# Building the scan part's diagonals by small transfers, ordering its transfers as written, and moving the skip term to TensorE

## The chip, the cores and the metric

The program runs on one core of a Trainium2 chip, in one launch. The metric is the device time of one execution in microseconds (us). The core's engines each run their own list of instructions in order: PE (TensorE, matrix products), DVE (VectorE), ACT (ScalarE), POOL (GpSimd) and SP (SyncE, which here only issues DMA transfers). Semaphores make one engine wait for another.

## The reference, cut to what matters

Two layers run one after the other on an image of 8 x 128 channels x 128 x 128. The first (Fourier and convolution attention) is untouched by the change. The second is a selective state-space layer over the 16,384 places of each image:

```python
xs, z = split(u @ W_in)                  # u: normalised image, 256 + 256 channels
xc = silu(depthwise_conv4(xs) + conv_b)
dt, Bm, Cm = split(xc @ W_xproj)         # 8, 16, 16 numbers for each place
delta = softplus(dt @ W_dt + b_dt)
# for every place t, 256 channels d, 16 states n:
h[d,n] = exp(delta[d] * A[d,n]) * h[d,n] + delta[d] * xc[d] * Bm[n]
y[d]   = sum_n h[d,n] * Cm[n]
y = (y + xc * D_param) * silu(z)
out = x + y @ W_out
```

`xc * D_param` is the skip term and `silu(z)` is the gate.

## The kernel before, in words

The second layer is the stage at L1025 to L1390, here called the scan part. It works on chunks of T = 512 places, 32 chunks for each of 8 images, 256 in all. A chunk `i` has ST = 16 steps. A step `n` handles one block of 128 partitions (32 channels x 4 groups of states, with 2 states of each group at a time), with h (half of the channels) from s // 8, mp (which pair of states) from s // 4 % 2 and k from s % 4. The steps of one chunk thus use mp = 0, 1, 0, 1 in fours.

In each step the main loop (L1366 to L1390) writes, in this order: `keep_state(n-1)` (ACT copies the last state), `product(n+1)` (PE writes delta * xc * Bm into an `hb` tile in PSUM), the functions of the list `first`, `decay(n+3)` (ACT takes two exponentials `dA`), `scan(n)` (DVE runs two scans of 512 places), the functions of the list `beside`, and `weigh(n)` (POOL multiplies the 2 x 512 results by Cm). An entry `(step, rel, f)` of a list means: in this step call f for chunk i + rel. Entries with rel 1 and 2 prepare later chunks, those with 0 and -1 finish the current and the last one.

`product` (L1239) is 32 small matmuls. Its moving operand `bd` holds, for each block of 64 places, a diagonal matrix with the values of Bm on the diagonal, and its stationary operand is `duT`, the transposed delta * xc. `hb` has two buffers, so `product(n+1)` must wait until `scan(n-1)` is through. A float32 matmul stands in the profile as two MATMUL records, so one product is 64 records.

Before the change the diagonals are made by multiplying the constant `same` (64 x 64 ones on the diagonal) by Bm: six on DVE (`diagonals`, L1198, 128x512 each) and sixteen on ACT (`more_diagonals`, L1210, 128x64 each) for each chunk. `keep_b` (DVE, L1193) keeps a copy of Bm from PSUM.

`add` (L1273) sums over the states on PE: 32 matmuls for each chunk, in groups of four that use different columns of the array, into bank 3 of PSUM (`y`). `skip` (DVE, L1288) then computes xc * D_param + y into `yt` in SBUF, and `gated` (POOL, L1297) multiplies `yt` by the gate `sz`. `project` (PE) and `residual` (DVE) end the chunk.

The other parts of the preparation are `conv` (PE, eight matmuls of 128x512, four taps for each half), `conv_act` (ACT), `gate` (PE and ACT), `xproj` and `xproj_act` (PE and ACT, tile `dbl`), `step_sizes` (PE, tile `e_dt`), `step_sizes_act` (ACT, tile `dl`), `drive` (POOL, tile `du`), `turn` (PE transposes, tile `e_t`) and `turn_b` (PE transposes of Bm, tile `e_bt`).

Some values must be repeated over partitions, which goes through DRAM: `cd` holds Cm and is read back as `crep` (4 transfers of 128 KB for each of the two mp), and `dld` holds delta and is read back as `dlrep` (4 transfers of 256 KB for each half). `xin` is the chunk's input. `acc` is a block of 32 image rows read in pieces of 128 bytes (2 MB, once in 8 chunks); it takes the result, and `out<-acc` writes it back the same way from ACT's queue.

PE, DVE, ACT and POOL are wrapped in `InOrder` (L169), which keeps each engine's instructions in the order in which the program writes them. All their instructions therefore have the helper's line, L180, in the profile. The transfers of SP are not wrapped before the change: the scheduler of the framework chooses their place.

Of the kernel before, what the change touches and what calls it, by code (L numbers as in the profile page):

```python
# [27 lines left out]
T = 512  # L28
# [83 lines left out]
def _layout(a):  # L112
# [46 lines left out]
    o["same64"] = np.tile(np.eye(64, dtype=np.float32), (2, 1))  # L159
# [31 lines left out]
def tile_kernel(ctx: ExitStack, tc: tile.TileContext, I: dict, out: bass.AP):  # L191
# [833 lines left out]
    with tc.tile_pool(name="e_c", bufs=1) as cp, tc.tile_pool(name="e_w", bufs=2) as wk, tc.tile_pool(  # L1025
# [10 lines left out]
        same = fixed("same", [128, ND], I["same64"])  # L1036
        unit = fixed("unit", [128, 128], I["consts"][:, 0:128])
        win = fixed("win", [128, 2 * DI], I["win"])
# [4 lines left out]
        conv_b, b_dt, d_par = dv[:, 0:2], dv[:, 2:4], dv[:, 4:6]  # L1043
        A = fixed("A", [128, NM, NBK], I["alog"])
# [3 lines left out]
        wf = cp.tile([128, 4, DI], F32, name="wf")  # L1048
        nc.sync.dma_start(wf.rearrange("p a d -> p (a d)"), I["cw"].partition_broadcast(128))
        for k in range(4):  # L1050
            nc.vector.tensor_tensor(wf[:, k, :], wf[:, k, :], win[:, 0:DI], ALU.mult)
        state = cp.tile([128, NM, NBK], F32, name="state")
        ch = {}
# [4 lines left out]
        pe, dve, act, gps = (InOrder(tc, e) for e in (nc.tensor, nc.vector, nc.scalar, nc.gpsimd))  # L1058

        def load(i):  # L1060
            b, k = divmod(i, NCH)
            xin = wk.tile([128, T], F32, name="xin")
            nc.sync.dma_start(xin, X1[b, :, k * T : (k + 1) * T])
            ch[i] = {"xin": xin}

        def rows_of(b, r0):

            t = wk.tile([128, W, QR], F32, name="acc")
            nc.sync.dma_start(t, X1[b].rearrange("c (w h) -> c w h", h=H)[:, :, r0 : r0 + QR])
            image[b, r0] = t  # L1070
# [34 lines left out]
        def conv_act(i):  # L1105
            c = ch[i]
            c["xc"] = wk.tile([128, 2, T], F32, name="xc", bufs=3)
            for h in range(2):
                act.activation(c["xc"][:, h, :], c.pop(("xcp", h)), AF.Silu, bias=conv_b[:, h : h + 1])

        def gate(i):
            c = ch[i]
            c["sz"] = wk.tile([128, 2, T], F32, name="sz", bufs=3)
            for h in range(2):
                ps = bank("e_z", h)
                pe.matmul(ps, lhsT=win[:, DI + h * 128 : DI + (h + 1) * 128], rhs=c["u"][:, 3:], start=True, stop=True)
                act.activation(c["sz"][:, h, :], ps, AF.Silu)

        def xproj(i):
            c = ch[i]  # L1120
            ps = c["xp"] = bank("e_x", 0)
            for h in range(2):
                pe.matmul(ps, lhsT=wx[:, h, :], rhs=c["xc"][:, h, :], start=(h == 0), stop=(h == 1))

        def xproj_act(i):
            c = ch[i]
            c["dbl"] = wk.tile([128, T], F32, name="dbl", bufs=1)
            act.copy(paired(c["dbl"]), halves(c.pop("xp")))
            d = c["cd"] = dp.tile([DS, T], F32, name="cd")
            for x in range(2):  # L1130
                nc.sync.dma_start(halves(d)[:, x], paired(c["dbl"][64 + DS : 96, :])[:, x])
            repeat_c(i, 0)

        def repeat_c(i, mp):

            t = ch[i]["c", mp] = wk.tile([128, 2, T], F32, name="crep", bufs=3)
            for q in range(NQ):
                m = NM * q + 2 * mp
                to = t[q * NR : (q + 1) * NR].rearrange("p m t -> p (m t)")
                nc.sync.dma_start(to, ch[i]["cd"][m : m + 2].rearrange("m t -> (m t)").partition_broadcast(NR))  # L1140
# [8 lines left out]
        def step_sizes_act(i):  # L1149
            c = ch[i]  # L1150
            c["dl"] = wk.tile([128, 2, T], F32, name="dl", bufs=1)
            d = dp.tile([2, 128, T], F32, name="dld")
            for h in range(2):
                act.activation(c["dl"][:, h, :], c.pop(("dp", h)), AF.Softplus, bias=b_dt[:, h : h + 1])
            nc.sync.dma_start(d.rearrange("h p t -> p h t"), c["dl"])
            for h in range(2):
                if h:
                    repeat_c(i, 1)
                t = c["dlr", h] = wk.tile([128, 4, T], F32, name="dlrep")
                for q in range(NQ):  # L1160
                    nc.sync.dma_start(t[q * NR : (q + 1) * NR], d[h].rearrange("(k r) t -> r k t", r=NR))
# [7 lines left out]
        def turn(i, part):  # L1169

            c = ch[i]
            ps = c["tp"] = bank("e_t", 1)
# [20 lines left out]
        def keep_b(i):  # L1193
            c = ch[i]
            c["bt"] = wk.tile([128, NTB, DS], F32, name="bt")
            dve.tensor_copy(c["bt"], c["bp"][:, : NTB * 32].rearrange("p (j n) -> p j n", n=32)[:, :, :DS])

        def diagonals(i, mp, j):  # L1198
# [3 lines left out]
            if (mp, j) in ((0, 0), (1, 0)):  # L1202
                c["bd", mp] = wk.tile([128, NTB, NQ, ND, 2], F32, name="bd")
            to = [128, NQ, ND, 2]
            b = c["bp"][:, 32 * j : 32 * j + DS].rearrange("p (q m) -> p q m", m=NM)[:, :, 2 * mp : 2 * mp + 2]
            dve.tensor_tensor(
                c["bd", mp][:, j], same.unsqueeze(1).unsqueeze(3).to_broadcast(to), b.unsqueeze(2).to_broadcast(to), ALU.mult
            )

        def more_diagonals(i, which):  # L1210

            c = ch[i]
            for n in which:
                j, q, m = 2 + n // 8, n // 2 % 4, n % 2
                at = NM * q + 2 + m
                act.activation(c["bd", 1][:, j, q, :, m], same, AF.Identity, scale=c["bt"][:, j, at : at + 1])
# [56 lines left out]
        def add(i, g, *js):  # L1273

            if g % 2 == 0 and 0 in js:
                ch[i]["y", g // 2] = bank("y", 3)
            for j in js:
                for k in range(4):
                    pe.matmul(
                        ch[i]["y", g // 2][k * NR : (k + 1) * NR, :], lhsT=gath, rhs=hcs[ST * i + 4 * g + k][:, j, :],  # L1280
                        start=(g % 2 == 0 and j == 0), stop=(g % 2 == 1 and j == 1), skip_group_check=True,
# [6 lines left out]
        def skip(i, h):  # L1288

            c = ch[i]  # L1290
            if h == 0:
                c["yt"] = wk.tile([128, 2, T], F32, name="yt", bufs=1)
            dve.scalar_tensor_tensor(
                c["yt"][:, h, :], c["xc"][:, h, :], d_par[:, h : h + 1], c.pop(("y", h)), ALU.mult, ALU.add
            )

        def gated(i, h):  # L1297
            yt = ch[i]["yt"][:, h, :]
            gps.tensor_tensor(yt, yt, ch[i]["sz"][:, h, :], ALU.mult)

        def project(i):
            c = ch[i]
            ps = c["o"] = bank("e_o", 1)
# [3 lines left out]
        def residual(i):  # L1307
# [12 lines left out]
            (0, 1, lambda i: conv(i, 1, 2)),  # L1320
            (0, 0, lambda i: diagonals(i, 1, 1)),
            (0, 0, lambda i: more_diagonals(i, range(6, 11))),
            (1, 1, lambda i: conv(i, 1, 3)),
            (1, 0, lambda i: more_diagonals(i, range(11, 16))),
            (2, 1, conv_act),
            (2, -1, lambda i: add(i, 3, 0, 1)),
            (3, -1, lambda i: skip(i, 1)),
            (4, -1, lambda i: gated(i, 1)),
            (4, 1, xproj),
            (5, 1, xproj_act),  # L1330
            (5, 0, lambda i: add(i, 0, 0)),
            (6, 0, lambda i: add(i, 0, 1)),
            (6, 1, step_sizes),
            (6, 2, norm),
            (7, 1, turn_b),
            (8, -1, project),
            (8, 1, lambda i: drive(i, 0)),
            (8, 1, keep_b),
            (9, -1, residual),
            (9, 1, lambda i: drive(i, 1)),  # L1340
            (9, 2, lambda i: conv(i, 0, 0)),
            (10, 0, lambda i: add(i, 1, 0, 1)),
            (11, 0, lambda i: skip(i, 0)),
            (11, 1, lambda i: diagonals(i, 0, 0)),
            (11, 1, lambda i: turn(i, 0)),
            (11, 2, lambda i: conv(i, 0, 1)),
            (12, 0, lambda i: gated(i, 0)),
            (12, 1, lambda i: turn_act(i, 0)),
            (12, 1, lambda i: diagonals(i, 0, 1)),
            (12, 2, lambda i: conv(i, 0, 2)),  # L1350
            (13, 1, lambda i: diagonals(i, 0, 2)),
            (13, 1, lambda i: turn(i, 1)),
            (13, 2, lambda i: conv(i, 0, 3)),
            (14, 1, lambda i: turn_act(i, 1)),
            (14, 1, lambda i: diagonals(i, 0, 3)),
            (14, 0, lambda i: add(i, 2, 0, 1)),
            (15, 1, lambda i: diagonals(i, 1, 0)),
            (15, 1, lambda i: more_diagonals(i, range(6))),
            (15, 2, lambda i: conv(i, 1, 0, 1)),
        ]  # L1360
        first = [
            (3, 1, gate),
            (7, 1, step_sizes_act),
        ]
        LEAD = 3
        for n in range(-2 * ST, (total + 1) * ST):  # L1366
            i, s = divmod(n, ST)
            if s == 0:
                if there(i + 2):
                    load(i + 2)  # L1370
# [37 lines left out]
```

## Time and profile before

| what | value |
|---|---|
| median of 3 runs | 18526.35 us (18518.2 to 18531.05) |
| the profiled execution's own time | 18481.4 us |
| its span | 18479.6 us |
| stretch 6580 to 18480 us, the scan part: PE busy | 10919 of 11900 us |
| the same: DVE busy | 11240 of 11900 us |
| the same: POOL busy | 10868 of 11900 us |
| the same: ACT busy | 9519 of 11900 us |
| the same: granted TensorE clock | 0.98 |
| the same: DMA share, rate | 0.45, 100 GB/s |
| 0 to 6580 us, the first layer: DMA share, rate | 0.68, 215 GB/s |

A busy share tells how long an engine held at least one instruction. PE is pipelined and the end of a matmul is modelled, so neighbouring records overlap a little, and the distance from one group's start to the next is the better duration. In a group's row the two numbers after the bar are its busy time in us and the mean length of one instruction in ns. What follows the second bar is the idle time of the engine just before such instructions, with the releaser that ended it; "issue" means that no semaphore explains the idle time. The DMA share is a sum over packets, so it can pass 1 where an engine has several in flight.

### The profile page before, as it was taken

Reading aid. Unit: us, or ns where it says so; the run is one execution under the profiler, and the core shown is the slowest. Engines: PE = TensorE matmul, PEld = TensorE weight load, DVE = VectorE, ACT = ScalarE, POOL = GpSimd, SP = SyncE. Lnnn points to the kernel's source line nnn. Section 1 sums busy time; section 2 is a strip of 40 time slices with the busy share of each in tenths; the row PEclk is TensorE's granted clock in tenths of the full one; section 3 lists DMA queues with packets and bytes.
Section 4 is the critical chain, followed back from the end, with each engine's and each line's share of the span. In section 5 each row is a group of like instructions: output and inputs, shape, how many; then the busy total and the mean of one; then the engine's idle time right before and its main releaser. Section 6 shows DMA issues by size and latency. Waiting matters only on the chain.

```text
span 18479.6 us, 790974 instructions
## 1 busy us (share of the span) xinstructions
PE 16503.3 (89%) x353336; PEld 9529.9 (52%) x353336; DVE 14244.2 (77%) x15987; ACT 12009.6 (65%) x26077; POOL 13090.9 (71%) x7572
## 2 busy tenths in 40 slices
PE   7789988888888889999999999999999999999998
PEld 5566665566555544444444444444444444444444
DVE  5544544334444479999999999999999999999999
ACT  4443434334233358778778878888888878887887
POOL 3333334444222269999999999999999989998998
PEclk8889999988999999999999999999999999999999
DMA  9963337777776654444454445444544454445443
GB/s 375 371 235 89 96 106 248 240 230 218 207 204 192 186 139 100 103 96 100 97 105 101 100 96 108 99 99 98 106 98 99 100 103 100 99 98 105 98 98 88
DMA packets 2434566, 2601.34 MB, mean 141 GB/s; under 512 B 1221965, under 2 KB 1624013, under 8 KB 2396866
## 3 DMA queue, kind: packets, MB, share of 16 engines
q1 hardware_dynamic: 1730850, 2206.28, 43.9%
q10 hardware_dynamic: 679840, 277.32, 7.1%
q0 software_dynamic: 20480, 67.13, 1.1%
q8 instruction: 2783, 45.60, 1.1%
q14 instruction: 613, 5.02, 0.1%
HBM read 1715.23 MB, written 834.93 MB: 138 GB/s over the span
## 4 chain that ended last, share of the span: by engine, by line
PE 56%; DVE 22%; DMA 8%; issue 7%; ACT 6%; POOL 1%; SPq 1%; DVEq 0%; ACTq 0%; POOLq 0%
DVE hs L180 15%; PE hb L180 14%; PE y L180 8%; PE c_mm L180 6%; PE e_xc L180 4%; DVE bd L180 3%; PE e_z L180 3%; PE e_x L180 3%; PE d_b L180 2%; PE a_mm L180 2%; DMA d_of<-OFL 2%; PE c_gram L180 2%; PE d_p L180 2%; DMA X<-d_x 2%; ACT L180 2%
## 5 line engine op out<-in xcount | busy, mean ns | idle before, releaser
L180 POOL TENSOR_TENSOR hc<-hs,crep 128x1024 f32<-128x1024 f32 x4096 | 9653.4, 2377 | 982.4 <-DVE hs L180 858.1
L180 DVE TENSOR_TENSOR_SCAN hs<-dA,state,hb 128x512 f32<-128x512 f32 x7936 | 9611.4, 1269 | 558.2 <-PE hb L180 418.8
L180 PEld LDWEIGHTS hb<-bd,duT 64*32 64x32 f32 x262144 | 3727.5, 106 | 3971.3 <-issue 2808.4
L180 PE MATMUL hb<-bd,duT 64*32 64x128 f32 x262144 | 4919.3, 275 | 798.9 <-issue 417.8
L180 ACT ACTIVATE dA<-dlrep,A 128x512 f32<-128x512 f32 x8192 | 5443.8, 714 | 59.6 <-DMA dlrep<-dld 51.6
L180 PE MATMUL e_xc<-u,wf 128*128 128x512 f32 x4096 | 2263.9, 646 | 34.1 <-DVE A L1046 20.8
L180 PE MATMUL y<-hc,gath 128*32 128x512 f32 x16384 | 2053.4, 601 | 32.5 <-issue 31.2
L180 ACT COPY state<-hs 128x2 f32<-128x2 f32 x4096 | 775.9, 189 | 1676.2 <-DVE hs L180 1649.5
L180 ACT ACT_TABLE_LOAD x1057 | 1356.1, 1283 | 75.0 <-PE e_dt L180 40.1
L180 PE MATMUL c_mm<-src,taps 32*32 32x512 f32 x32768 | 1211.5, 626 | 191.8 <-issue 158.7
L180 DVE COPY vst<-c_mm 128x512 f32<-128x512 f32 x1024 | 685.0, 689 | 717.4 <-PE c_mm L180 620.6
L180 ACT ACTIVATE bd<-same,bt 128x64 f32<-128x64 f32 x4096 | 1054.0, 339 | 0.8 <-PE hb L180 0.8
L180 DVE TENSOR_TENSOR bd<-same,e_bt 128x512 f32<-128x512 f32 x1536 | 1036.7, 675 | 0.0
L180 PEld LDWEIGHTS c_mm<-src,taps 32*32 32x32 f32 x32768 | 681.2, 105 | 683.7 <-issue 493.5
L180 POOL TENSOR_SCALAR qm<-vst,cst 128x512 f32<-128x512 f32 x256 | 505.4, 2070 | 745.4 <-DVE vst L180 745.2
L180 ACT ACTIVATE junk<-vst 128x256 f32<-128x256 f32 x1024 | 416.4, 410 | 923.0 <-DVE vst L180 921.9
L180 PE MATMUL a_mm<-xt,wp 128*128 128x256 f32 x3072 | 760.6, 409 | 264.5 <-ACT pk L180 184.1
L180 POOL TENSOR_TENSOR eo<-eo,et 128x1008 f32<-128x1008 f32 x128 | 298.8, 2334 | 969.3 <-DVE et L180 960.8
L180 POOL DMA_DIRECT2D X<-d_x x256 | 139.1, 543 | 1069.5 <-DVE d_x L180 939.9
L180 PEld LDWEIGHTS e_xc<-u,wf 128*128 128x128 f32 x4096 | 654.7, 194 | 440.2 <-issue 436.1
L180 DVE TENSOR_TENSOR d_x<-d_p,d_x 128x512 f32<-128x512 f32 x256 | 274.9, 1074 | 780.3 <-DMA d_x<-in_x 490.0
L180 PEld LDWEIGHTS a_mm<-xt,wp 128*128 128x128 f32 x3072 | 619.3, 205 | 421.7 <-ACT pk L180 194.6
(179 smaller groups left out, 20011.2 us busy)
## 6 DMA issues: line engine op xcount, KB each, us to landing
dlrep<-dld SPq DMA_DIRECT2D x2048, 256.0 KB
crep<-cd SPq DMA_DIRECT2D x2048, 128.0 KB
dld<-dl SPq DMA_DIRECT2D x256, 512.0 KB
src<-Pq SPq DMA_DIRECT2D x128, 544.5 KB
src<-Pv SPq DMA_DIRECT2D x128, 544.5 KB
src<-Pk SPq DMA_DIRECT2D x128, 544.5 KB
src<-Px SPq DMA_DIRECT2D x128, 544.5 KB
xt<-in_x SPq DMA_DIRECT2D x64, 1024.0 KB
```

The costliest lines, as they stand in the source:

```text
L180: made = method(*args, **kwargs)
```

## The change

The change touches the scan part and its constants. It does these things:

1. The diagonals are no longer computed. Four DRAM tiles `diag` (2 chunks by parity x 2 mp, 1 MB each) are set to zero once. `keep_b`, now on ACT, copies Bm to SBUF, and four SP transfers for each chunk write it onto the diagonals in DRAM, 1024 pieces of 8 bytes each. `load_b` reads one `diag` tile (1 MB) back as `bd`, twice for each chunk; `bd` gets three buffers.
2. The transfers of SP are wrapped in `InOrder`, so they are issued as written.
3. Most preparation of a chunk comes about two steps earlier, and `load` one chunk ahead of where it was. Pairs of matmuls that stood together are split over two steps (`add` of groups 1 to 3, `xproj`, `gate`), and `repeat_sizes` gets entries of its own.
4. The skip term becomes a matmul with a diagonal matrix `dd` of D_param (128x128), which starts the accumulation of `y`. `skip` goes away, and `gated` becomes one DVE multiplication that reads `y` from PSUM.
5. Some buffers change: `xin` has one, `xc` two; `e_t`, `e_o` and the first half of the gate use bank 2 of PSUM.

```diff
+    diag = {(n, mp): dram.tile([128, DROW], F32, name=f"diag{n}{mp}") for n in range(2) for mp in range(2)}
...
+        zero = zp.tile([128, DROW], F32, name="zero")
+        nc.gpsimd.memset(zero, 0.0)
+        for d in diag.values():
+            nc.sync.dma_start(d, zero)
...
+        for h in range(2):
+            nc.vector.tensor_scalar(dd[:, h, :], unit, d_par[:, h : h + 1], None, ALU.mult)
...
-        pe, dve, act, gps = (InOrder(tc, e) for e in (nc.tensor, nc.vector, nc.scalar, nc.gpsimd))
+        pe, dve, act, gps, sp = (InOrder(tc, e) for e in (nc.tensor, nc.vector, nc.scalar, nc.gpsimd, nc.sync))
...
         def keep_b(i):
-            dve.tensor_copy(c["bt"], c["bp"][:, : NTB * 32].rearrange("p (j n) -> p j n", n=32)[:, :, :DS])
+            act.copy(bt, c.pop("bp")[:, : NTB * 32].rearrange("p (j n) -> p j n", n=32)[:, :, :DS])
+            for mp in range(2):
+                d = diag[i % 2, mp]
+                for x in range(2):
+                    ap = [[DROW + 2, ND], [2 * ND, NTB * NQ], [1, 2]]
+                    to = bass.AP(d.tensor, d.offset + x * ND * DROW, ap)
+                    frm = bt[ND * x : ND * x + ND].rearrange("p j (q m) -> p (j q) m", m=NM)[:, :, 2 * mp : 2 * mp + 2]
+                    sp.dma_start(to, frm)
+        def load_b(i, mp):
+            t = ch[i]["bd", mp] = wk.tile([128, NTB, NQ, ND, 2], F32, name="bd", bufs=3)
+            sp.dma_start(t.rearrange("p j q t m -> p (j q t m)"), diag[i % 2, mp])
...
                 ch[i]["y", g // 2] = bank("y", 3)
+                pe.matmul(ch[i]["y", g // 2], lhsT=dd[:, g // 2, :], rhs=ch[i]["xc"][:, g // 2, :], start=True, stop=False, skip_group_check=True)
...
-            dve.scalar_tensor_tensor(
-                c["yt"][:, h, :], c["xc"][:, h, :], d_par[:, h : h + 1], c.pop(("y", h)), ALU.mult, ALU.add
-            )
-            gps.tensor_tensor(yt, yt, ch[i]["sz"][:, h, :], ALU.mult)
+            dve.tensor_tensor(c["yt"][:, h, :], c.pop(("y", h)), c["sz"][:, h, :], ALU.mult)
```

The new lists, with the entries of a step in written order:

```python
beside = [(0, 1, conv_act), (0, 1, gate(0)), (1, -1, add(3, 0)), (2, -1, add(3, 1)), (2, 1, xproj(0)),
    (3, 1, xproj(1)), (3, -1, gated(1)), (3, 1, xproj_act), (4, 1, turn_b), (4, 1, step_sizes), (4, 2, norm),
    (4, 1, keep_b), (5, 0, add(0, 0)), (5, 1, repeat_sizes(0)), (6, 0, add(0, 1)), (6, 1, drive(0)),
    (6, 1, load_b(0)), (7, 1, drive(1)), (7, -1, project), (8, -1, residual), (8, 2, conv(0, 0)),
    (9, 0, add(1, 0)), (9, 2, conv(0, 1)), (9, 1, turn(0)), (10, 0, add(1, 1)), (10, 2, conv(0, 2)),
    (10, 1, turn_act(0)), (10, 1, load_b(1)), (11, 0, gated(0)), (11, 1, repeat_c(1)), (11, 2, conv(0, 3)),
    (11, 2, conv(1, 0)), (12, 1, repeat_sizes(1)), (12, 3, load), (12, 1, turn(1)), (12, 2, conv(1, 1)),
    (13, 0, add(2, 0)), (13, 1, turn_act(1)), (14, 0, add(2, 1)), (14, 2, conv(1, 2)), (15, 2, conv(1, 3))]
first = [(1, 1, gate(1)), (5, 1, step_sizes_act)]
```

## The prediction, on record before the run

> **What bounds the kernel now.** I read the page's busy shares first, then stretches of the scan part, then single chunks on the timeline.
>
> ```profile
> PE 16503.3 (89%) x353336; PEld 9529.9 (52%) x353336; DVE 14244.2 (77%) x15987; ACT 12009.6 (65%) x26077; POOL 13090.9 (71%) x7572
> ```
>
> In the scan part (stretch 11000 to 12000; busy time of PE, PEld, DVE, ACT, POOL, then the granted clock, DMA share and GB/s) three engines are near full, so none may be called the bound from its share:
>
> ```profile
> 11000.00:12000.00 1000.00, 920.95 (x24405) 479.07 (x24404) 948.66 (x910) 800.48 (x1706) 916.51 (x433) 0.98 0.47 101
> ```
>
> From one `e_bt` to the next, a chunk takes 46.30 us on average and 44.85 at the median of 219, counted from the timeline. PE, steps 1 to 6 of a chunk (start, length):
>
> ```profile
> 12040.86 1.99 PE L180 MATMUL e_z<-u,win 128*128 128x512 f32 x4
> 12042.77 1.16 PE L180 MATMUL hb<-bd,duT 64*32 64x128 f32 x64
> 12043.86 1.98 PE L180 MATMUL e_x<-xc,wx 128*128 128x512 f32 x4
> 12045.78 1.16 PE L180 MATMUL hb<-bd,duT 64*32 64x128 f32 x64
> 12046.86 1.07 PE L180 MATMUL y<-hc,gath 128*32 128x512 f32 x8
> 12047.86 1.16 PE L180 MATMUL hb<-bd,duT 64*32 64x128 f32 x64
> ```
>
> PE has no pause here: start to start gives 1.91 us for `e_z` and `e_x` (two matmuls), 1.09 for a product, 1.00 for a `y` of 8 records. Elsewhere DVE leads, where the diagonals stand between the scans:
>
> ```profile
> 12018.54 0.68 DVE L180 TENSOR_TENSOR bd<-same,e_bt 128x512 f32<-128x512 f32 x1
> 12019.13 2.44 DVE L180 TENSOR_TENSOR_SCAN hs<-dA,state,hb 128x512 f32<-128x512 f32 x2
> 12021.49 0.66 DVE L180 TENSOR_TENSOR bd<-same,e_bt 128x512 f32<-128x512 f32 x1
> ```
>
> A pair of scans takes 2.36 us start to start, a diagonal 0.58; the same view gives 0.65 for `skip`, 1.04 for `residual`, 0.12 for the copy of Bm.
>
> DVE for a chunk: 16 x 2.36 + 6 x 0.58 + 2 x 0.65 + 1.04 + 0.12 = 43.7 us. PE: 16 products 17.44; `y` 2 x 1.00 + 3 doubles of 1.85 = 7.55; `e_z`, `e_x`, `e_o` 3 x 1.91 = 5.73; `e_dt` 1.06; `e_bt` 0.36; the eight conv matmuls as one pair 1.91, four alone at 1.06 and two joined to an `e_t` at 1.44, 9.03; sum 41.2. I set the two lists side by side, step by step, with two distances from the timeline: a product can start 0.14 us after the end of the scan two steps back, a scan starts 1.31 us after its product. PE then waits for DVE in steps 1, 2, 11, 13 and 14, 3.4 us in all, and the period is 41.2 + 3.4 = 44.6. Quiet chunks on the timeline take 44.6 to 45.0, so this account holds. The other 1.7 us of the mean are disturbances. The table of waits (8000 to 18000, 216 chunks; us, times, longest) names the largest on PE:
>
> ```profile
> PE hb L180 <- issue: 366.7, 253, 4.4
> PE hb L180 <- DVE hs L180: 291.5, 455, 1.2
> PE y L180 <- issue: 26.7, 18, 3.0
> PE e_xc L180 <- issue: 9.6, 6, 2.1
> ```
>
> "issue" here is PE stopping within a product's 64 records, where nothing in the program waits: 403 / 216 = 1.9 us for each chunk. Its code comes by DMA (queue 8, 16 KB packets of 1.15 us, about nine for each chunk), and the pauses fall where data moves. Of those inside products, 238 of 242 follow 4 us with a DMA share above 0.4: 0.0004 us of pause for each us of time below 0.4, 0.024 from 0.4 to 0.8, 0.16 above 0.8 (my count over the timeline and the packet records). The 2 MB of `acc` (issued at 12214) show it:
>
> ```profile
> 12215.00:12220.00 5.00, 4.05 (x112) 2.07 (x108) 5.00 (x5) 4.61 (x11) 4.42 (x2) 1.00 1.24 187
> 12220.00:12225.00 5.00, 3.86 (x105) 1.97 (x106) 3.06 (x5) 1.77 (x4) 2.97 (x3) 1.00 1.65 146
> 12230.00:12235.00 5.00, 5.00 (x78) 2.22 (x76) 2.45 (x2) 3.86 (x10) 2.60 (x2) 0.66 0.80 73
> ```
>
> PE's count falls from about 145 to 105 in 5 us, and after a pause the clock is 0.66 (12230): the `e_x` there took 3.62 us instead of 1.98. At a mean clock of 0.985 this is 0.6 us for each chunk.
>
> **The change, part by part.**
>
> *Diagonals off DVE and ACT.* DVE loses 6 x 0.58 and the copy, 3.6 us for each chunk; ACT loses 16 `bd` activations of 339 ns (about 4.1 us start to start) and gains one short copy. ACT had 20% idle: worth nothing by itself.
>
> *Skip and gate.* `skip` becomes a DVE product from PSUM, priced like the diagonal that reads PSUM too (0.6 against 0.65). POOL loses 2 x 1.24 and goes from 42.5 to 40.0 (16 x 2.34 + 2 x 1.26). PE gains two 128x512 matmuls, each between groups of another shape, so 1.06 as a lone `e_xc`: +2.1.
>
> *Splits.* Three double `y` become six singles (+0.45); `e_z` and `e_x` become four lone matmuls, 4.24 instead of 3.82 (+0.4). The fixed 0.15 to 0.2 us of a group is paid once more for each.
>
> So PE: 17.44 + 8 x 1.00 + 2.12 + 4.24 + 1.91 + 1.06 + 0.36 + 9.03 = 44.2; DVE: 37.8 + 2 x 0.6 + 1.04 = 40.0. **PE becomes the bound.** Side by side again, every product finds its scan ended 0.4 to 2.4 us earlier: no wait is left, and no slack either. A quiet chunk takes 44.2 against 44.6, and every pause of PE counts in full, where before 3.4 us of waits absorbed part (1.9 + 0.6 of stalls cost 1.7).
>
> *Moved preparation, new waits.* The second `gate` needs bank 1, free after `conv_act`: a table load (1.28), two activations (1.15) and two `dA` (1.24) after PE's step 0 starts, 3.7 against PE's arrival at 3.24; ACT is up to 1.4 ahead, so 0 to 0.45: I take 0.2. Other preparation stands one step or more ahead of its use. On SP the written order is `cd`, `crep`, `diag`, `dld`, `dlrep`, two `bd`, `crep`, `dlrep`, `xin`. The second `bd` waits for step 11's product, the `crep` behind it for step 11's `weigh`, the `dlrep` for step 12's exponentials; all have nine steps (25 us) to their use, against some 13 us of transfers. Only in a chunk with `acc` (18 us, now first in the step 0 queue) do `dlrep` and `bd` land near 36 to 40 us, due at 36 and 41: 0 to 5 us in 8 chunks, I take 0.2 for each chunk.
>
> *Transfers.* New for each chunk: 4096 packets of 8 bytes and 2.1 MB of `bd`. Packets of 8 bytes are not in this trace. The nearest are 4-byte completions (12.8 ns) and 128-byte reads (22.4); the 128-byte writes of queue 10 take 0.044 x 10000 x 16 / 442800 = 15.9 ns:
>
> ```profile
> q1 hardware_dynamic: 899061, 913.45, 39.5%
> q10 hardware_dynamic: 442800, 56.62, 4.4%
> ```
>
> That makes 3.3 to 5.7 us of 16 engines, 4.1 taken. The 2.1 MB take 5.6 us at the first slices' 375 GB/s, 9.9 at the 212 of a `dlrep` burst; 7 taken. Together 11 us (8.9 to 15.6) beside the present 0.44 x 46.3 = 20. Were all of it at a share over 0.8, 11 x 0.16 = 1.8 us of new pauses; were it spread, 0. I take 0.8.
>
> [...]
>
> *Once:* four 1 MB zero writes ahead of the first chunk, 4.2 MB at 375 to 200 GB/s, 11 to 21 us; 15 taken.
>
> **Sum for a chunk:** 44.2 + 0.2 + 0.2 + 1.9 (pauses as now) + 0.8 + 0.6 (clock) = 47.9 against 46.3; 256 x 1.6 + 15 = +425. Against the profiled execution's 18,481 that is 18,906. The median of the runs is 45 above it; on its scale I predict 18,950, +2.3%. Bounds: stalls and waits of 2.4 (pauses 1.9, clock 0.5, all else nothing), 46.6, 18,620; 44.65 + 0.6 + 1.9 + 2.5 + 0.8 = 50.5 at worst, 19,600.
>
> **Rivals.**
>
> *DVE sets the pace.* For: its 95%. Then 43.7 - 40.0 = 3.7 us for each chunk: 18,526 - 947 = 17,580. Against: PE's sum of 44.2 alone forbids it, unless groups of different shape overlap. 4%.
>
> *Faster, PE paced but calm.* The transfers now stand earlier and apart; if that brings pauses, clock and waits under 2.1 us in all, the sign turns. At 1.2: 45.4, 18,526 - 230 + 15 = 18,310. For: late `dlrep` and `out` collisions cost up to 7 us in one of 8 chunks now. Against: half as much DMA time again. 16%.
>
> *Same,* between the two: 9%.
>
> *The queue overflows.* If 8-byte pieces cost five times a 128-byte write (80 ns, 20 us of 16 engines), the queue holds 20 + 20 + 7 = 47 us for each chunk and itself sets the pace, 47 to 50: 19,400. Against: size hardly matters from 4 to 128 bytes. 12%.
>
> *The forecast* (46.6 to 48.9): 59%.
>
> The range of 18,400 to 19,300 leaves out the first rival and parts of the calm and the overflowing case. Faster by over 0.2%: 20%; within 0.2% (what a measurement can tell from no change): 9%; slower: 71%.
>
> **What would show it.** Right: PE's share in the scan part rises above 93% while DVE's falls below 88%; "PE hb <- DVE hs" nearly vanishes; "issue" exceeds 1.9 us for each chunk; quiet chunks take 44 to 45. Wrong: DVE over 93%; `e_z` to `hb` under 1.0; pauses below 1.2; or `hb` waiting for `bd` transfers.

## The result and the profile after

The changed kernel takes 19,404.8 us (median; 19,398.3 to 19,418.7), the kernel before on the same chip 18,528.7: ratio 1.0474, 95% interval 1.0456 to 1.0493. The prediction had the sign and said 18,950; the measured time lies above its range, which ended at 19,300.

The page's busy line of the changed kernel, and its stretch 11000 to 12000 (same columns as before):

```profile
PE 17397.3 (90%) x354360; PEld 9603.2 (50%) x354360; DVE 13446.4 (69%) x14197; ACT 11092.3 (57%) x22237; POOL 12477.1 (64%) x7061
```

```profile
11000.00:12000.00 1000.00, 922.52 (x22855) 449.46 (x22844) 818.51 (x704) 675.15 (x1286) 804.52 (x363) 0.98 0.66 140
```

DVE fell from 0.95 to 0.82 and POOL from 0.92 to 0.80, so they did get the room that the change meant to give. PE's share did not rise: it is 0.92 as before, with 6% fewer instructions in the same time. DMA went from 0.47 to 0.66. The waits of the changed kernel, 8000 to 18000, 202 chunks (us, times, longest):

```profile
DVE hs L179 <- PE hb L179: 1479.1, 1149, 6.7
...
PE hb L179 <- issue: 592.0, 465, 5.0
...
PE hb L179 <- DMA bd<-diag: 77.1, 25, 4.8
```

"PE hb <- DVE hs", 291.5 us before, is gone from the large entries; now DVE waits for PE. PE itself waits for nothing that the program asks of it, except for `bd` 25 times, once for each `acc`. What it has instead is "issue", 592 us against 367 in fewer chunks.

Where the 918.5 us between the two profiled spans stand, counted from one `e_bt` to the next:

| | before | after | difference |
|---|---|---|---|
| up to the first product | 6608.8 | 6643.6 | +35 |
| the two chunks in eight that `acc` touches, together | 97.4 | 108.9 | 32 x 11.5 = +368 |
| each of the other six (called ordinary below) | 45.4 | 48.1 | 192 x 2.7 = +518 |

The usual distances of PE's groups, start to start on the timeline, add up to 43.86 us for an ordinary chunk, and chunks of e1 below, which has the same list, take that when no pause falls into them (the kernel before: 44.6). So PE's list did get shorter than the old loop, and 4.3 us of other things were added to it. Here is one of them, in PE's timeline of the changed kernel:

```profile
12092.31 0.94 PE L179 MATMUL hb<-bd,duT 64*32 64x128 f32 x48
12095.03 0.45 PE L179 MATMUL hb<-bd,duT 64*32 64x128 f32 x16 [1.78 <-issue]
12095.42 1.07 PE L179 MATMUL y<-hc,gath 128*32 128x512 f32 x8
```

The product stops after 48 of its 64 records for 1.78 us; nothing in the program separates record 48 from 49. Such pauses inside products add up to 1.98 us for each chunk before and 3.46 after (8000 to 18000; counted from the start of one record to the start of the next, which is more than the idle times of the table of waits). In ordinary chunks they are 1.3 and 2.7, and no chunk of this window is free of pauses any more.

SP's timeline of the changed kernel, one chunk (start, time to issue, number):

```profile
12018.25 0.77 SPq L179 DMA_DIRECT2D cd<-dbl  x2
12020.29 3.46 SPq L179 DMA_DIRECT2D crep<-cd  x4
12023.85 4.03 SPq L179 DMA_DIRECT2D diag<-bt  x4
12027.98 0.61 SPq L179 DMA_DIRECT2D dld<-dl  x1
12033.73 1.75 SPq L179 DMA_DIRECT2D dlrep<-dld  x4
12035.57 0.85 SPq L179 DMA_DIRECT2D bd<-diag  x2
12040.53 1.72 SPq L179 DMA_DIRECT2D crep<-cd  x4
12042.36 6.27 SPq L179 DMA_DIRECT2D dlrep<-dld  x4
12048.70 0.40 SPq L179 DMA_DIRECT2D xin<-X  x1
```

The writes take SP 4 us, and `dld`, which stands behind them, must land before the first `dlrep` is issued; so this one starts at 12033.7. From there 4.75 MB follow each other without a gap: at the median of the ordinary chunks the DMA share stays above 0.75 for 17 us (5.5 before; running mean of 2 us).

In a chunk with `acc` a second thing happens. PE's timeline:

```profile
12241.58 1.13 PE L179 MATMUL e_xc<-u,wf 128*128 128x512 f32 x2
12247.26 1.66 PE L179 MATMUL hb<-bd,duT 64*32 64x128 f32 x64 [4.55 <-DMA bd<-diag]
12248.85 2.07 PE L179 MATMUL e_xc<-u,wf 128*128 128x512 f32 x2
```

and SP's own waits of the same kernel:

```profile
SPq L179 <- DMA out<-acc: 358.9, 25, 18.1
```

The kernel before had the same wait at the `dlrep` of L1161, where it was shorter:

```profile
SPq L1161 <- DMA out<-acc: 226.9, 27, 11.9
```

SP had issued `dlrep` at 12224.2 and stood until 12242.3: the program gives the transfers of SP and ACT eight completion semaphores in turn (100 and 102 to 108 in the trace), and SP's next transfer waited for the one that `out<-acc` (2 MB in pieces of 128 bytes) still held. Everything written behind it waited too, and PE stood 4.55 us for `bd`. The `e_xc` behind it takes 2.07 us instead of 1.13, so the clock fell as well. Behind the pause of 1.78 us above the rows keep their length. In the kernel before, the rows keep theirs behind a pause of 2.09 us, but behind one of 2.00 us `e_x` takes 3.62 us instead of 1.98:

```profile
12221.14 0.64 PE L180 MATMUL hb<-bd,duT 64*32 64x128 f32 x24 [2.09 <-issue]
12221.71 1.92 PE L180 MATMUL y<-hc,gath 128*32 128x512 f32 x16
...
12229.19 0.92 PE L180 MATMUL hb<-bd,duT 64*32 64x128 f32 x45 [2.00 <-issue]
12230.04 3.62 PE L180 MATMUL e_x<-xc,wx 128*128 128x512 f32 x4
```

In the clock records of the changed kernel (8000 to 18000) the clock fell within 7 us of 24 of the 70 pauses of 1.5 to 2 us that began at full clock, of 42 of 73 of 2 to 3 us and of 45 of 47 longer ones. So in this kernel it fell behind short pauses too, though less often than behind long ones. The stretches at half clock in this window add up to 464 us, against 287 us before.

### The profile page after: what moved, and what is told of

Read it like the earlier page. It is cut to its first block, busy times and chain, and to the rows that moved or that the text cites. A ratio compares the mean times of both kernels' runs of the same rounds, so it can differ in the third digit from the quotient of the medians.

```text
span 19398.1 us, 788686 instructions
## 1 busy us (share of the span) xinstructions
PE 17397.3 (90%) x354360; PEld 9603.2 (50%) x354360; DVE 13446.4 (69%) x14197; ACT 11092.3 (57%) x22237; POOL 12477.1 (64%) x7061
## 4 chain that ended last, share of the span: by engine, by line
PE 79%; DMA 9%; issue 6%; DVE 3%; ACT 2%; POOL 1%; SPq 0%; POOLq 0%; DVEq 0%; ACTq 0%
PE hb L179 24%; PE y L179 13%; PE e_xc L179 10%; PE c_mm L179 6%; PE e_z L179 3%; PE e_x L179 3%; PE e_o L179 2%; PE d_b L179 2%; DMA d_of<-OFL 2%; DMA out<-acc 2%; PE a_mm L179 2%; PE c_gram L179 2%; PE d_p L179 2%; PE d_a L179 1%; PE e_t L179 1%
## 5 line engine op out<-in xcount | busy, mean ns | idle before, releaser
L179 PE MATMUL hb<-bd,duT 64*32 64x128 f32 x262144 | 5127.3, 278 | 894.4 <-issue 768.2
L179 PEld LDWEIGHTS hb<-bd,duT 64*32 64x32 f32 x262144 | 3806.7, 107 | 4203.1 <-issue 3517.6
L179 PE MATMUL y<-hc,gath 128*32 128x512 f32 x16384 | 2243.2, 610 | 46.0 <-issue 42.9
L179 ACT ACTIVATE sz<-e_z 128x512 f32<-128x512 f32 x512 | 306.1, 598 | 865.0 <-PE e_z L179 864.5
L179 PEld LDWEIGHTS y<-hc,gath 128*32 128x32 f32 x16384 | 336.6, 108 | 929.6 <-issue 600.4
## 6 DMA issues: line engine op xcount, KB each, us to landing
crep<-cd SPq DMA_DIRECT2D x2048, 128.0 KB
```

The lines of the kernel that those rows point to most:

```text
L179: made = method(*args, **kwargs)
```

## The experiments

The first theory was the prediction's, with a larger price: PE's list is full, so every pause counts, and the new transfers bring more of them. What is it about the transfers: the 8-byte writes, the reads, their amount, or where they stand? Where `diag` is not written, its tiles hold values of x, and Bm is left out.

**e1, e2, e3: without the new transfers, without the writes, without the reads.**

```diff
-                    sp.dma_start(to, frm)                                   # e1, e2
-            sp.dma_start(t.rearrange("p j q t m -> p (j q t m)"), diag[i % 2, mp])   # e1, e3: a fixed tile
```

> The changed kernel with neither the 8-byte writes nor the two reads of 1 MB: two bd tiles are filled once from a piece of the input, so Bm is left out of the product. Theory (TensorE sets the pace, and the added transfers cost it time by holding up its code): issue 43.9 us for each chunk, pauses back to about 2, clock and waits 0.7, together 46.6 instead of 49.7; 256 x 3.1 = 790 us less, 18,610. Rival (the added TensorE work alone is the loss, transfers are hidden): no more than 0.5% less, 19,300 or above.

> The changed kernel without the 8-byte writes; the two reads of 1 MB stay (the diag tiles hold a piece of the input, Bm is left out). Theory: the 4096 small packets take 2.0 us of the 16 engines, the reads 5.6; about a quarter of the loss by transfers goes, 0.8 us for each chunk, 19,200. Rival (the small pieces are the trouble, by count and not by bytes): most of it goes, 2.5 us for each chunk, 18,760.

> The changed kernel with the 8-byte writes, without the two reads of 1 MB: bd is filled once from a piece of the input (Bm is left out of the product). Theory: 5.6 of 7.6 us of new transfer time go, 2.3 us for each chunk, 18,820. Rival (small pieces are the trouble): 19,300 or above.

Measured: e1 18,335.5 (ratio to before 0.9891, 0.9873 to 0.9909), e2 18,592.0 (1.0025, 1.0012 to 1.0037), e3 18,428.0 (0.9936, 0.9916 to 0.9957). Against e1 the writes alone cost 92 us, the reads alone 257, both together 1,069. So neither is dear by itself; the cost is not a sum. e1 also shows the most that the change could have brought in this form, with the skip term on PE: diagonals that cost nothing on any engine gain 1.1%, because PE's list of 43.86 us stands behind the old 44.6.

**e4: the skip term back on DVE and the gate on POOL, in the changed kernel.**

```diff
-                pe.matmul(ch[i]["y", g // 2], lhsT=dd[:, g // 2, :], rhs=ch[i]["xc"][:, g // 2, :], start=True, ...)
+            dve.scalar_tensor_tensor(c["yt"][:, h, :], c["xc"][:, h, :], d_par[:, h : h + 1], c.pop(("y", h)), ALU.mult, ALU.add)
+            gps.tensor_tensor(yt, yt, ch[i]["sz"][:, h, :], ALU.mult)
```

> The changed kernel with the skip term on VectorE and the gate on GpSimd again, as before the change (xc gets its third buffer back, the exponentials have 9 buffers instead of 10). Theory: TensorE's list is 2.1 us shorter and it is the bound, so 47.6 us for each chunk, 256 x 2.1 = 540 us less, 18,870. Rival (the transfers set the pace and TensorE only waits for them): within 0.5%, 19,310 to 19,500.

Measured 19,399.3 (1.0469, 1.0446 to 1.0493): two matmuls less for each chunk, 2.1 us, gain nothing. PE's pauses took much of their place, 4.35 us for each chunk instead of 3.46; the stretches at half clock grew from 464 to 717 us and the waits for `bd` from 77 to 132. The row of the table of waits (in 201 chunks; us, times, longest):

```profile
PE hb L179 <- issue: 744.8, 522, 5.5
```

With this "PE's list is the bound" falls as an account of the changed kernel by itself. It looks as if something else gave the pace of the chunk and PE's pauses filled what is left; this run does not show what.

**e5, e6: the same transfers spread, and bunched.** The new theory was the unbroken block: PE's code comes by DMA, and in 17 us at a full share it comes late. e5 moves the second `bd` read behind the second `dlrep` and the second `crep` to step 15. e6 is e2 (no writes) with the first `dlrep` moved behind the second `bd`.

```diff
-            (10, 1, lambda i: load_b(i, 1)),        # e5: behind (12, 1, repeat_sizes(1))
-            (11, 1, lambda i: repeat_c(i, 1)),      # e5: to step 15
-            (5, 1, lambda i: repeat_sizes(i, 0)),   # e6: behind (10, 1, load_b(1))
```

> The changed kernel, all transfers kept, their order on SP changed: the second bd read comes after the second dlrep (step 12), the second crep at step 15 with two buffers instead of three, so that it waits for the chunk's last weigh. New theory (what costs is the unbroken block of 17 us in which dlrep, both bd reads, crep and dlrep follow each other and TensorE's code waits in between; not the amount): the longest block is about 9 us, pauses fall from 3.5 to about 2 us for each chunk, period 46.6, 18,600. Rival (the amount of transfers sets the loss): 19,300 to 19,450.

> e2_no_small_writes with the first dlrep moved behind the second bd read in SP's order, so that bd, dlrep, crep and dlrep stand together again; the same bytes and packets as e2 (no 8-byte writes; bd holds a piece of the input, Bm is left out). New theory (the block): pauses back to 3 us or more, 19,100 to 19,400. Rival (the small writes themselves are needed for the loss, by their number or as writes just before the reads): as e2, 18,600.

e5 took 22,334.6 (1.2083, 1.2058 to 1.2107). It tested something else than meant: `crep` at step 15 waits for that step's `weigh`, and the next chunk's `cd`, writes, `dld`, `dlrep` and `bd` stand behind it in SP's written order (162 chunks):

```profile
ACT dA L179 <- DMA dlrep<-dld: 2934.5, 163, 20.6
...
PE hb L179 <- DMA bd<-diag: 2064.2, 163, 15.4
```

e6 took 19,446.8 (1.0521, 1.0503 to 1.0539): with e2's bytes, and 1.0521 against 1.0025 by the ratios to the kernel before. Pauses are 3.58 us for each chunk (e2: 1.90). So the order of the transfers alone can cost what the change costs. Not all of e6 is PE's code: its `dlrep` is later, and "PE hb <- ACT duT" adds 0.66 us for each chunk. But all of that wait lies in one chunk of eight, next to `acc`. The ordinary chunks have none of it and take 48.5 us against the 45.6 of e2.

**e7, e8: the diagonals by DMA in the kernel before; the changed kernel with SP's order left to the scheduler.**

```diff
+            (8, 1, lambda i: write_b(i)), (11, 1, load_b(0)), (15, 1, load_b(1))     # e7, on the kernel before
-        pe, dve, act, gps, sp = (InOrder(tc, e) for e in (..., nc.sync))             # e8: sp = nc.sync
```

> The kernel before with the diagonals by DMA alone: the 8-byte writes after keep_b at step 8, the bd reads at steps 11 and 15, SP's order left to the scheduler, the skip term on VectorE and the gate on GpSimd, nothing moved up. VectorE's list falls from 43.7 to 40.2 us, TensorE's stays at 41.2. New theory: good if the block stays short: 44.6 to 45.5 us, about 18,250; with a long block 47 or more, 18,800. Rival (the amount of transfers sets the loss): 48 us, 19,000 or above.

> The changed kernel with SP's transfers left to the scheduler (not held in written order), all else kept. New theory: if the written order makes the block, the scheduler's order brings it down to 18,700 or less; if the block stands there too, 19,400 again. Rival (amount): 19,400 whatever the order is. The trace tells the length of the block.

e7 took 20,463.9 (1.1072, 1.1052 to 1.1091). PE waits 5.2 us for each chunk for `bd`: without the earlier preparation the round trip through DRAM is late. That the first part of the change needs the third is the likely reading; `bd` also has two buffers here instead of three, and this was not varied alone. e8 took 19,117.7 (1.0349, 1.0333 to 1.0365), by the ratios 1.2% less than the changed kernel. The run at a high share is as long (19.5 us) and an ordinary chunk nearly so (47.8). Most of its gain lies in the chunks around `acc` (the three next to it take 152 us instead of 157), so that is where the written order costs, more than in the ordinary ones.

**e9, e12, e13: all bytes kept, the block broken.** e9 puts the writes behind the first `dlrep` and the second `bd` last. e12 takes both `crep` early and holds the second `bd` in a buffer of its own until step 14. e13 also moves the second `dlrep` behind it.

```diff
+            (6, 1, write_b), (8, 1, load_b(0)), (12, 1, load_b(1))                    # e9
+            (4, 1, repeat_c(1)), (6, 1, write_b), (8, 1, load_b(0)), (15, 1, load_b(1))   # e12
+            (8, 3, load), (15, 1, repeat_sizes(1))                                    # e13, with e12's
```

> The changed kernel with the same transfers in another written order, in which nothing queues behind a late release as in the spread of step 15: the four diagonal writes stand behind the first dlrep (step 6 instead of 4), the first bd read at step 8 and the second behind the second dlrep at step 12; order cd, crep, dld, dlrep, diag, bd, crep, dlrep, bd, xin. All bytes are kept. Block theory (the cost is one unbroken stretch of 17 us at a full DMA share, in which PE's code comes late): the first dlrep falls away from the block, its longest run above a share of 0.75 drops to 10 us or less, pauses fall from 3.5 to 2.3-2.8 us for each chunk, the time to 18,800-19,100; the acc chunks stay slow, since the transfers behind out<-acc are still in order. Rival (the sum of bytes at this demand sets the time, whatever the order): 19,300-19,500. If the block stays as long (13 us or more) the run says nothing about the theory beyond that it stays near 19,400.

> The changed kernel with the same transfers and bytes, set apart so that no queue position waits for a late release: both crep at steps 3 and 4 (four crep buffers), dld and the first dlrep at step 5, the four diagonal writes at step 6, the first bd at step 8, the second dlrep and xin at step 12, the second bd in a buffer of its own that holds it until step 14 (bd0 two buffers, bd1 one; dA nine, bt one to make room). The late-writes run left an unbroken run of 12.5 us at a DMA share over 0.75 and paid like the changed kernel, so it did not tell length from bytes. Here bd, dlrep and bd stand 3 us or more apart and the longest run should be 5 to 8 us. Block theory (pauses and lateness come from one unbroken run of over some 10 us, not from the bytes): pauses 1.6-2.3 us for each chunk as in the kernels with runs of 5 to 8 us, period 46.3-47.5, time 18,500-18,850. Rival (all bytes together, 31 us of 16 engines for each chunk, set the pauses however they stand): pauses 3.0 or more and 19,200-19,500.

> The former kernel (e12) with the second dlrep moved behind the second bd read at step 15 and xin behind the first bd read at step 8; all bytes kept. In e12 the first bd read waited for the landing of the writes, so that bd, dlrep and xin still stood together for 10.5 us at a share over 0.75. Here the longest run in an ordinary chunk should be 8 us or less (bd with dlrep, 2 MB). In every kernel so far a stretch at a full DMA share cost PE under 0.1 us of pause for each us in its first 4 to 6 us, and 0.2 to 0.5 from then on. Block theory: pauses fall below 2.3 us for each chunk and ordinary chunks to 46-47 (they took 47.8-48.7 in the changed kernel and in e12); the chunks with acc stay bad, 53 and 56 to 62, as what is late there is the second bd; time 18,800-19,200. Rival (bytes, whatever their order): pauses of 3 or more, ordinary chunks 48 and over, 19,300-19,600.

Measured: e9 19,567.0 (1.0582, 1.0565 to 1.0598), longest run about 12.5 us; e12 19,602.4 (1.0621, 1.0603 to 1.0639), 10.5 us; e13 19,601.0 (1.0614, 1.0596 to 1.0631), 6.5 us. In all three an ordinary chunk takes 48.1 to 48.6 with 3.3 to 3.6 us of pauses. e13 has short runs and pays as before: the length of the run is not the cause. This theory falls as well.

**e10, e11: the skip term on TensorE in the kernel before; the same with two DVE diagonals on POOL.**

```diff
+                pe.matmul(ch[i]["y", g // 2], lhsT=dd[:, g // 2, :], ...)
+            if (mp, j) in ((0, 3), (1, 0)): e, b = gps, c["bt"][:, j, :]              # e11
```

> The kernel before with the fourth part of the change alone: the skip term as a TensorE matmul that starts y, the gate multiplied from PSUM on DVE, POOL without gated; diagonals on DVE and ACT as before. By the account of engine lists PE has 41.2 + 2.1 = 43.3 us and DVE stays at 43.7, POOL 40.0; the two lists then wait for each other less or more depending on place, quiet chunks 44.8 to 46, pauses as before (2.0): 18,500-18,900. The rival, that PE paces with no absorption, gives 43.3 + 3.4 + 1.7 = 48.4 and 19,060; that POOL's relief frees the loop gives 18,400 or less.

> The former one, with two of the six DVE diagonals (the last of mp 0 and the first of mp 1) computed on POOL from the SBUF copy of Bm. DVE 43.6 - 1.2 = 42.4, POOL 40.0 + 2.4 to 3, PE 43.3 alike. If DVE's list between the scans holds the quiet chunk, the time falls below that of the former by 0.3 us or more for each chunk, to some 18,300-18,450, perhaps below the kernel before. If PE's list and its pauses hold it, it stays within 0.3% of the former.

e10 took 18,728.0 (1.0127, 1.0111 to 1.0144), e11 18,691.2 (1.0108, 1.0087 to 1.0129). The fourth part alone costs 1.3%: the quiet chunk goes from 44.6 to 45.6 us. PE has 2.1 us more, DVE no less, and each still waits for the other. The relief of DVE in e11 gives half a us of the quiet chunk (45.1) and 0.2% of the time, with intervals that overlap.

**e14, e15, e16: place against bytes, and half of each.** e14 is e13 without the writes (the bytes of e2). e15 is the changed kernel with half of the writes, e16 with one of the two reads.

```diff
-            (6, 1, write_b),                              # e14, on e13
-            for mp in range(2):                           # e15: range(1)
+            if mp: ch[i]["bd", mp] = bds; return          # e16, in load_b
```

> The order of the former kernel (e13), without the 8-byte writes (Bm is left out: the diag tiles hold values of x from the start); the bytes of e2. Byte theory (pauses follow the sum of the transfers): like e2, pauses 1.6-2.2 us for each chunk, ordinary chunks 45.3-46, 18,500-18,700. Position theory (what costs is a bd and a dlrep of 2 MB standing together in steps 14 to 1, which paid 2 us of pause in e13): pauses 2.8 or more, ordinary chunks 47.5 and over, 19,200 or more.

> The changed kernel with half of the 8-byte writes: those of mp 0 stay, those of mp 1 go (its diag tiles hold values of x, so this half of Bm is left out); all reads stay. Half-way in transfers between e2 (18,592) and the changed kernel (19,405). If the cost rises evenly with the demand, about 19,000. If it sets in as a step once the transfers close up, either 18,500-18,700 or 19,300-19,400.

> The changed kernel with one of the two bd reads: mp 0 is read, mp 1 uses a fixed tile (this half of Bm is left out); all writes stay. Half-way in transfers between e3 (18,428) and the changed kernel (19,405), and the unbroken block loses 1 MB. If the cost rises evenly with the demand, about 18,900. If it is a step, either 18,400-18,600 or 19,250-19,400.

e14 took 19,443.6 (1.0530, 1.0514 to 1.0545): the bytes of e2 and the cost of the changed kernel (some of its buffers differ from e2's too, `bd` and `crep` among them). e15 took 18,577.0 (1.0056, 1.0037 to 1.0074), e16 18,566.6 (1.0054, 1.0039 to 1.0069): half of either takes away nearly all of the loss. With one point between none and all, the cost looks like a step, and e2 against e6 shows that the side a kernel falls on depends on place. On one side ordinary chunks take 44.5 to 45.8 us (e1, e2, e3, e15, e16), on the other 47.8 to 48.6 (the changed kernel, e4, e6, e8, e9, e12, e13, e14); the kernel before, e10 and e11 take 45.4 to 46.3, and e5, e7, e17 and e18, with waits of their own, 50.4 and more.

SP's timeline of e15, a kernel on the good side, shows the one regularity that I found between the sides:

```profile
12003.58 1.75 SPq L179 DMA_DIRECT2D dlrep<-dld  x4
12005.49 3.29 SPq L179 DMA_DIRECT2D bd<-diag  x2
12014.01 2.59 SPq L179 DMA_DIRECT2D crep<-cd  x4
12016.70 1.80 SPq L179 DMA_DIRECT2D dlrep<-dld  x4
```

Here `crep` and `dlrep` come 8.5 us after `bd`, and the mean DMA share dips to 0.49 between them (e2: 0.35, e16: 0.54); from the issue of `crep` on, the pauses of an ordinary chunk then come to 0.3 us in e2 and 0.5 in e15. In the changed kernel `crep` is issued 5 us after `bd` (12040.53 and 12035.57), the share stays at 0.99, and the pauses from there to the end of the block come to 2.5 us. In e16 `crep` follows 6 us after its one `bd`, and they come to 0.9 us. In e14 the other `bd` read stands directly ahead of a `dlrep`, in steps 14 and 15:

```profile
12010.94 0.32 SPq L179 DMA_DIRECT2D bd<-diag  x1
12011.31 2.21 SPq L179 DMA_DIRECT2D dlrep<-dld  x4
```

That pair alone costs 1.9 us. In the order `dlrep`, then `bd`, the reads cost 0.9 (e14, and e2 and e15 with the second `bd` behind it). This was read out of the traces afterwards; no run changed it by itself.

**e17, e18: large transfers in parts of 128 KB, and the same with the skip term on DVE.** Lining up the code fetches of PE with its instructions (below) suggested that they wait behind what is already issued. With the eight semaphores, parts of 128 KB leave 1 MB under way at most (8 x 128 KB, `acc` apart).

```diff
+            for r in range(0, 128, 16):
+                sp.dma_start(t[r : r + 16], diag[i % 2, mp][r : r + 16])
```

> The changed kernel, everything in its order and with all its bytes, but with its large transfers cut into parts of 128 KB by partitions: each bd read in 8 parts, each dlrep in 8 instead of 4, dld in 4, xin in 2. The program gives SP's and ACT's transfers eight completion semaphores in turn, so no more than eight can be under way, and parts of 128 KB hold what is issued and not landed to about 1 MB (2 MB with acc). In the traces so far a PE code fetch starts over 150 instructions late in 0 to 1% of cases with under 0.05 MB under way, 10-30% up to 0.5 MB, 10-60% from 0.5 to 1 MB, 40-90% from 1 to 2 MB (kernel before: never over 0.9 MB; changed kernel: up to 2.7). Theory of the queue (a code fetch starts late by what is already issued ahead of it): pauses 1.6-2.4 us for each chunk, ordinary chunks 45.3-46.5, time 18,550-18,900. Rival (place and sum of the transfers, not what is under way at a time): 19,200 or more; the more issues on SP (about 45 for each chunk) then make it rather worse.

> The former kernel with the skip term on DVE and the gate on POOL as in e4 (xc three buffers, dA nine). PE's list is 41.7 us, DVE's 40.1, POOL's 42.5, so all three have slack if the transfers leave PE alone. Theory of the queue: 44.2-45.5 for each chunk, 18,000-18,500, below both kernels. Rival: as e4, 19,200 or more.

Neither came near what the theory of the queue gives: 20,428.5 (1.1081, 1.1056 to 1.1105) and 20,439.6 (1.1084, 1.1060 to 1.1108). The parts move more slowly: a `bd` packet of 8 KB takes 879 ns, against 351 in the changed kernel. The queue's share of e17, 8000 to 18000, against 58.1% in the changed kernel:

```profile
q1 hardware_dynamic: 1673961, 1180.83, 77.2%
```

The DMA is now at a full share for close to 30 us of each chunk, pauses are 4.6 us, and PE waits another 478 us for `bd` in 71 waits. By that count the amount under way is smaller, and the pauses are not, so this amount is not the cause by itself either. As the cut also lengthened the time at a full share, the run does not exclude that it matters.

**What the pauses are.** This can be read from the traces. PE's code is fetched over queue 8 in packets of 16 KB, one for each 254 records of PE, matmuls and weight loads counted together. In six traces (before, the changed kernel, e1, e2, e6, e12), PE resumes 1.4 to 1.5 us (median) after the end of such a fetch. Counting how many PE records have begun when a fetch starts, against the earliest fetches around it, gives its lateness. The fetch that ends a pause starts about 180 records late in the changed kernel (median; 5 to 95%: 108 to 244), while half of all fetches are under 72 (the figures move by some 30 with the stretch that is taken for the earliest). Why they start late shows when fetch starts are counted by the time since a large read was issued. Their mean is 0.19 for each us. In the kernel before, from 1 to 5 us after the first of four `dlrep` (1 MB) it is 0.02 to 0.07, and then 0.47. In e14, after the issue of a `bd` that stands beside a `dlrep` (2 MB), it is 0.01 to 0.09 from 1 to 6 us. In the changed kernel, whose mean is 0.18, it is 0.06 to 0.14 from 1 to 6 us after the first of four `dlrep`. So while one of these reads is moved, few code fetches begin. PE takes one each 5.2 us (1924 in the 10,000 us of the kernel before). That a hole of 4 us is mostly covered and one of 6 is not is a reading of these counts; no run varied the length of the hole alone.

| kernel | time, us | ordinary chunk | two with `acc` | pauses, us for each chunk |
|---|---|---|---|---|
| before | 18,529 | 45.4 | 97.4 | 1.98 |
| after | 19,405 | 48.1 | 108.9 | 3.46 |
| e1 no new transfers | 18,336 | 44.5 | 97.2 | 1.26 |
| e2 no writes | 18,592 | 45.6 | 99.2 | 1.90 |
| e6 e2, bunched | 19,447 | 48.5 | 109.1 | 3.58 |
| e14 e2's bytes, e13's order | 19,444 | 48.3 | 110.3 | 3.53 |
| e15 half the writes | 18,577 | 45.8 | 98.9 | 1.91 |
| e16 one read | 18,567 | 45.4 | 100.0 | 1.87 |
| e13 all bytes, short runs | 19,601 | 48.1 | 116.5 | 3.31 |
| e17 parts of 128 KB | 20,429 | 50.4 | 128.0 | 4.61 |

No kernel that does all of the work beats the kernel before.

## Why the prediction was right in sign and wrong in size

- *What the change takes off DVE and POOL* held: 0.82 and 0.80 in place of 0.95 and 0.92, and "PE hb <- DVE hs" vanished, as said.
- *PE's list of 44.2 us* was close: 43.86 measured. The terms for `dd` (1.06 each) and the splits held; `e_bt` with `e_dt` was counted at 1.42 and takes 1.07, since the two overlap.
- *The pieces of 8 bytes* were priced at 15.9 ns from the 128-byte writes; they take 7.9. The total of 11 us of new transfer time for each chunk held all the same (0.44 x 46.3 = 20.4 against 0.62 x 49.6 = 30.8), as the others became slower: a `bd` packet of 8 KB takes 351 ns, and the mean packet of 2 KB went from 132 to 159 ns.
- *The step that failed is the price of the transfers*: "Were it spread, 0. I take 0.8." In the window 8000 to 18000 the pauses in products rose by 1.5 us, and others, in `y` and between groups, by 0.2, so the term came to 1.7, near its upper bound of 1.8. By the idle times of the table of waits, which the prediction counted, it came to 1.4 (654 / 202 against 403 / 216). I had priced new DMA time by a mean rate, as if each us of it cost alike. Half of it costs almost nothing (e15, e16), the whole costs all. The same bytes cost 0.3% or 5.2% by order alone (e2, e6).
- *Behind it stands the sentence on SP*, that all transfers have nine steps to their use "against some 13 us of transfers". It asked whether each lands in time, and for PE, in ordinary chunks, each does. It did not ask what stands next to what once the writes, 4 us on SP, and the landing of `dld` have pushed the first `dlrep` towards `bd` and `crep`.
- *The clock* was kept at 0.6, though it falls behind pauses (45 of the 47 over 3 us above) and pauses were forecast to grow. By the prediction's own count it came to 1.15 us for each chunk (a mean clock of 0.977 from 8000 to 18000, 0.986 before). Of the 5.6 us between the list and the mean period of this window, pauses and waits explain 4.3; about 1.3 is left for slower groups, and the clock is most of that.
- *The chunks with `acc`* were given 0.2 us for each chunk. The wait for `bd` is 0.38, near enough, but the pair costs 11.5 us more (1.4 for each chunk), with the pauses and slow stretches that follow. So the second failed term is here: of the 494 us that the sum of 18,906 lacked against the profiled 19,400, some 265 lie in these 64 chunks and some 210 in the 192 others (the forecast gave each chunk 1.6 us). The two failed terms overlap, since part of what these chunks lose is pauses.
- *The signs*: DVE fell below 88%, "PE hb <- DVE hs" vanished and "issue" rose, as said for "right". PE's share stayed at 92% instead of passing 93%, no chunk was quiet any more, and a sign of "wrong" came, `hb` waiting for `bd`, 25 times. The prediction's own worst sum, 50.5 us and 19,600, did hold the result; the range was drawn at 19,300.
- *The rival "the queue overflows"* named nearly the time, 19,400, by a mechanism that did not occur: the pieces were cheap (7.9 ns) and the DMA share stayed at 0.6 to 0.66.
- *The calm rival* has its place in e1 and e3: paced by PE, 18,336 and 18,428. It needs the transfers that the change brings to be away.

Open remains what makes the step, that is, which neighbourhood of reads delays a second code fetch within the chunk. The rule of `crep` or `dlrep` close behind a `bd` fits the kernels on either side and was not varied alone.

## What to carry to other kernels

Here PE's code, long and unrolled, came by DMA, 16 KB for each 254 records, and its pauses inside products, which end 1.4 to 1.5 us (median) after a fetch, took 3.46 us of a chunk. So before moving work from an engine to DMA, look whether the engine that will set the pace stops inside groups ("issue"), and at how the large reads stand to each other (e2 and e6, the same bytes: 18,592 and 19,447 us), not only at the sum of bytes and at due times. First work out the ceiling: here free diagonals were worth 1.1%, against a risk of 5. With SP's transfers in written order, one that waited for a late event (`crep` in e5, 22,335 us), or for a semaphore that a slow transfer held (`out<-acc`, up to 18.1 us), made everything written behind it late.

## What the runs showed of the hardware that was not expected

- Scattered writes of 8 bytes were cheap: 7.9 ns of one DMA engine's time for each packet, half of a 128-byte write (15.9).
- Few code fetches started while a 1 MB read was moved: 0.02 to 0.07 for each us instead of 0.19 in the kernel before, 0.06 to 0.14 instead of 0.18 in the changed one.
- The loss did not grow evenly with the transfers: 18,567 to 18,592 us with half the writes, none, or half the reads, and 19,405 with all.
- The clock fell behind pauses of 1.5 to 2 us (24 of 70 in the changed kernel), not only behind long ones (45 of 47 over 3 us).
- In parts of 128 KB (16 rows of `bd`) the same reads were slower: SP's queue took 77.2% of the DMA time for 118 MB in each ms, with whole reads 58.1% for 128 MB.
